# A graph network with a mixture-of-experts layer: the shared output added by accumulating scatters, and four smaller reorderings

## The chip, the core and the metric

The kernel runs on one core of one Trainium2 chip. The core has five engines, each with its own instruction stream: TensorE (PE, matrix products, with PEld for its weight loads), VectorE (DVE), ScalarE (ACT), GpSimd (POOL) and SyncE (SP). [...] SP, and here also ACT, start plain transfers by DMA; POOL starts the indirect ones (gathers and scatters by row index). All of them move data through the same 16 DMA engines.

The metric is device time in microseconds, as the median of several runs. One further execution was recorded by the hardware profiler; every duration quoted here is from that record.

## The reference

There are 625 nodes with 1024 features each and 10625 directed edges (5000 random pairs in both directions and one self-loop for each node).

```python
def sage(h, W_self, W_neigh, b):            # mean over incoming edges
    agg  = segment_sum(h[src], dst, N)
    mean = agg / max(degree, 1)[:, None]
    return h @ W_self + mean @ W_neigh + b

h = layernorm(x)
x = x + sage(relu(sage(h, *layer0)), *layer1)

f = layernorm(x)
scores = softmax(f @ gate_w.T)              # 8 experts
w = scores * (one of the two best experts)
for e in range(8):                          # 1024 -> 1408 -> 1024
    out += w[:, e] * ((silu(f @ gate_e.T) * (f @ up_e.T)) @ down_e.T)
shared = (silu(f @ sg.T) * (f @ su.T)) @ sd.T         # 1024 -> 176 -> 1024
out += sigmoid(f @ shared_gate.T) * shared
return x + out
```

All of it is in float32.

## The kernel before

The nodes are cut into five tiles of 125 rows (index `t`), the 1024 features into eight chunks of 128 (index `c`) or into two halves of 512 (`half`).

A recorder, `Rec`, takes each operation with the tiles that it reads and writes. When all are recorded it emits them in program order on each engine, and puts in front of an operation only the semaphore waits that its data need. So the order on every queue is the order of the code, SP's queue of transfers included: a transfer that waits for its buffer holds all transfers behind it on SP. The helpers `ts`, `tt`, `stt`, `copy` (VectorE, or ScalarE on request), `act` (ScalarE), `mm` and `mm_all` (TensorE), `load`, `load_rows` and `store_rows` (SP by default) record one operation each, so in the profile all VectorE `tensor_tensor` operations carry the line of `tt`, L486, and so on.

The stages, in order:

1. *Start* (L575 to L602). SP loads the edge lists, then the first tile of x, then the weights `wn0`, the other tiles, `ws0`, `wn1`. POOL makes index patterns (`iota`). VectorE turns the edge lists into float columns and normalizes the first tile (`layernorm`, whose `rsqrt` is a bit trick with three rounds of Newton's method).
2. *Counting the edges* (L606 to L769). The adjacency matrix is built by 85 products of one-hot matrices; VectorE makes each pair (`os`, `od`) in `edge_rows`, TensorE counts in `count`. A list, `plan`, mixes them by hand with the transposes of the normalized rows (`tr`) and their products with `wn0` (`rows_times`). A check value `ok_i` says whether the compact counting was exact. Each of PE, ACT and DVE reads it into a register (`read_reg`), gives its branch unit a hint of the coming switch (`hint`), and runs the switch, which holds a slow recount in one case and the normal path in the other.
3. *The two graph layers* (L783 to L827). In `sage` the second layer's result is added to x in `xr`, and the row is normalized into `xf`, which is stored to a scratch tensor `xfw` in DRAM for the experts' gathers.
4. *Shared expert and routing* (L832 to L1087). `shared_up` gives the shared expert's hidden rows and the routing logits `lg` of a tile, `shared_transpose` turns them, `shared_down` multiplies with the down weights into a PSUM bank. Its `finish` scales the bank by the sigmoid weight into one of eight half-row tiles `share` (ScalarE), adds `share` to `xr` (POOL, L863), and after the second half stores the finished rows to `out` (SP). The tiles are finished in different places of the code, three groups of them late (`early`, `later`). Between them VectorE picks the two best experts and works out each row's place in its expert's list (`dest_i`, `row_i`, `place`, `id_of`, `pr`), TensorE turns the places into row indices (`own_indices`), POOL gathers the first expert's rows from `xfw` into `rows` (zeroed before), and VectorE computes the register words (`word`) by which the engines choose among bodies for different numbers of rows.
5. *The eight experts* (L1265 to L1335). For each expert: gate and up products with `wg` (11 chunks of 1 MB), the gate, transposes, down products with `wd` (11 tiles of 512 KB), the weighting into `ys`, and an indirect scatter that adds `ys` to the rows of `out` in DRAM. SP loads the next expert's `wg` chunk by chunk as TensorE leaves the buffers, and the next expert's `wd` after the present one's down products. Each scatter waits for all scatters of the expert before; those of expert 0 wait for the stores of `out` (`out_stores`).

At the end of stage 4 each of the five engines gets a no-op that reads `cnt_i`, the largest count of an expert (L1084). It orders `cnt_i` before the register loads that stand after the experts, where an overflow path is chosen for experts with more than 512 rows.

The buffers are numbered slots of 4096 bytes in each partition. `wg` lies in slots 0 to 21, `wd` in 22 to 32. The stages before use the same slots: the shared down weights lie in 22 and 23, `share` in 24 to 27 and `pr` with its neighbours in 28 to 31, so that the first loads of expert 0's weights have to wait for the last readers of these. `ws1` was in slots 24 to 31 until the last `sage`.

Of the kernel before, what the change touches and what calls it, by code (L numbers as in the profile page):

```python
# [15 lines left out]
N = 625  # L16
# [30 lines left out]
NSLOT = 3 * FC  # L47
HEAD = 4
# [249 lines left out]
def gnn_moe(nc, x, src, dst, w_gnn0, w_gnn1, b0, b1, w_gu, w_down, ws_up, ws_down, out):  # L298
# [38 lines left out]
    nid16 = const("nid16", [TP, NT], HP)  # L337
    idx = const("idx", [128, NE, NTL], I32)
# [66 lines left out]
    p = space(slot(24), slot(28))  # L405
    share = [p(f"share{i}", [TP, BANK]) for i in range(8)]
# [12 lines left out]
    place = p("place", [TP, NT, NE])  # L419
# [120 lines left out]
    def rsqrt(lo, hi):  # L540


        h, q, r = (v[:, lo:hi] for v in (ln_h, ln_q, ln_r))
        ts(h, ln_mv[:, lo:hi, 1], EPS, 0.5, ALU.add, ALU.mult)
        ts(q.bitcast(I32), h.bitcast(I32), 1, None, ALU.logical_shift_right)
        ts(r.bitcast(I32), q.bitcast(I32), -1.0, float(0x5ef759df - 2 ** 31), ALU.mult, ALU.add)
        for _ in range(3):
            tt(q, r, h, ALU.mult)
            tt(q, q, r, ALU.mult)
            stt(r, q, -1.5, r, ALU.add, ALU.mult)  # L550
# [24 lines left out]
    load(src_i, src.rearrange("(p c) -> p c", c=EC))  # L575
    load(dst_i, dst.rearrange("(p c) -> p c", c=EC))
    load_rows(xa[:, 0, :], x[:TP, :])
    for c in range(KD):
        load(wn0[:, c, :], w_gnn0[KD + c])
# [9 lines left out]
    iota(node_f, [[TP, NT], [1, PART]], 0)  # L589
    iota(pid, [[0, 1]], 0, 1)  # L590
    iota(ident, [[1, 128]], 0)
    iota(nid, [[TP, NT]], 0, 1)
    memset(const_ones, 1.0, "POOL")
    memset(ones, 1.0, "POOL")
    copy(node16, node_f)
    copy(src_f, src_i)
    ts(dhi_i, dst_i, 830.0, None, ALU.mult)
    ts(dhi_i, dhi_i, 16, None, ALU.logical_shift_right)
    ts(dval_i, dhi_i, 3.0, 127.0, ALU.mult, ALU.add)
    ts(dval_i, dval_i, 23, None, ALU.logical_shift_left)  # L600
    copy(dst_f, dst_i)
    stt(dmod, dhi_i, -float(DIG), dst_f, ALU.mult, ALU.add)  # L602
# [34 lines left out]
    def advance(until):  # L637
        while until not in did:
            what, n = now = vector.pop(0)
            if what == "rows":  # L640
                assert n < NOH or ("count", n - NOH) in did
                edge_rows(n)
            elif what == "ln" and n == 0:
                ts(ident, ident, pid, None, ALU.is_equal)
                layernorm(hrow[0], xa[:, 0, :], 0)
                did.add(("normal", 0))
            elif what == "ln":
                for t in range(1, NT):
                    moments(xa[:, t, :], t)
                rsqrt(1, NT)  # L650
                normal(hrow[1], xa[:, 1, :], 1)
                did.add(("normal", 1))
            else:
                assert ("tr", n - 2) in did
                normal(hrow[n % 2], xa[:, n, :], n)
            did.add(now)
# [57 lines left out]
    rows_times(y0, 3, 1, h0T, wn0, "p_y")  # L714
    for eng in ("PE", "ACT", "DVE"):
        read_reg(eng, body, (eng, "count"), ok_i, 1)
    bodies = {(eng, "count"): [(1, None), (0, None)] for eng in ("PE", "ACT", "DVE")}
    hint("count", bodies, ("PE",))
    scaled(c16[:, :, :N])
    tr(NT - 1)  # L720
    rows_times(y0, NT - 1, 0, h0T, wn0, "p_y")
    hint("count", bodies, ("ACT", "DVE"))
# [54 lines left out]
    copy(nid16, nid)  # L777
    iota(power_i[:, 0, :], [[3, NE]], 127)
# [37 lines left out]
    def sage(t, half, q):  # L816
# [6 lines left out]
        if half:  # L823
            rsqrt(t, t + 1)
            for n in (0, BANK):
                normal(f[:, n:n + BANK], xr[:, t, n:n + BANK], t)
            xf_stores.append(store_rows(xfw[t * TP:(t + 1) * TP, :D], f))  # L827

# [26 lines left out]
    def shared_down(t, half, b):  # L855
        lo = half * BANK
        q, o = bank("p_downs", b)[:TP, :], xr[:, t, lo:lo + BANK]
        mm(q, [(hts[:, c, t * TP:(t + 1) * TP], wds[c][:, lo:lo + BANK]) for c in range(SC)])

        def finish():  # L860
            s = share[(2 * t + half) % len(share)]
            act(s, q, AF.Copy, scale=wt[:, t, NE:])
            k.op("POOL", lambda h: h.tensor_tensor(o, s, o, ALU.add), r=[s, o], w=[o])  # L863
            if half:
                out_stores.append(store_rows(out[t * TP:(t + 1) * TP, :], xr[:, t, :]))
        return finish
# [31 lines left out]
    early = [shared_down(0, half, half) for half in range(2)]  # L898
# [6 lines left out]
    for finish in early:  # L905
        finish()
# [55 lines left out]
    stt(place, row_i, -128.0, dest_i, ALU.mult, ALU.add)  # L962
    for j in range(NTL):
        stt(id_of[:, :, :, j], row_i, float(j), of_id, ALU.is_equal, ALU.mult)
# [84 lines left out]
    for j in range(3):  # L1049
        memset(rows[j], 0.0, "POOL")  # L1050
# [22 lines left out]
    for j in range(3, NTL):  # L1073
        memset(rows[j], 0.0, "POOL")
        gather(0, j, xf_stores)
    copy(cnt_f[:, :NE], pos[0:1, NT, :])
# [7 lines left out]
    for eng in ENGINES:  # L1084
        k.op(eng, lambda h: h.nop(), r=[cnt_i])
# [179 lines left out]
    for e in range(NE):  # L1265
# [10 lines left out]
        for s in range(SEG):  # L1276
# [25 lines left out]
            if e == s == 0:  # L1302
                for c in range(FC):
                    load(wd[c], w_down[0, c])
            if more:
                for c in range(4 * s, min(4 * s + 4, FC)):
                    load_gu(e + 1, c)
# [20 lines left out]
        if more:  # L1328
# [5 lines left out]
            for c in range(FC):  # L1334
                load(wd[c], w_down[e + 1, c])  # L1335
# [109 lines left out]
```

## Time and profile before

| | |
|---|---|
| runs | 1177.58, 1181.73, 1186.67 us (median 1181.73) |
| profiled execution: time | 1181.65 us |
| profiled execution: span of the engines' work | 1179.9 us |
| TensorE busy | 1130.6 us (96%), granted clock 0.98 in the mean |
| VectorE, ScalarE, GpSimd busy | 193.4, 99.2, 55.7 us |
| DMA | 183.82 MB, 156 GB/s in the mean |

The stages in the span: edge counting until about 110 us, the first graph layer until 219, the second until 421 (with the shared expert woven in), routing until 472, then the experts. Experts 0 to 7 begin their products at 472, 567, 608, 803, 862, 898, 1006 and 1111 us; the number of rows of an expert sets its length.

[...] A 512-column float32 product is issued each 0.43 us at the full clock and each 0.85 us at half.

In lines of a wait view, "PE p_gu L526 <- DVE dest L495: 6.7, 1, 6.7" reads: TensorE, before its products into `p_gu` at line 526, stood idle for 6.7 us in all, once, 6.7 at the longest, and what ended it last by the record was VectorE's operation at line 495 that writes `dest`. "issue" stands for idle time that nothing in the record explains. Where a line begins with two numbers, these are the start in the span and the duration, both in us.

### The profile page before, as it was taken

How to read it: one execution, taken by the hardware profiler on the slowest of the kernel's cores; microseconds unless marked ns; L12 is line 12 of the kernel's file. 1: busy time of each engine (PE TensorE's matmuls, PEld its weight loads, DVE VectorE, ACT ScalarE, POOL GpSimd, SP SyncE). 2: the span in 40 equal slices, each digit the busy share in tenths (PEclk: the TensorE clock that was granted, in tenths of full speed). 3: DMA queues.
4: the chain of work that ended last, by engine and by line, in shares of the span. 5: the costliest groups of instructions: out<-in, count | busy, mean ns of one | idle time of the engine just before them, and what ended most of it. 6: DMA issues, size and time to landing. Idle time of an engine off the chain costs nothing.

```text
span 1179.9 us, 10473 instructions
## 1 busy us (share of the span) xinstructions
PE 1130.6 (96%) x4199; PEld 637.9 (54%) x4199; DVE 193.4 (16%) x590; ACT 99.2 (8%) x199; POOL 55.7 (5%) x57
## 2 busy tenths in 40 slices
PE   6999999999999996999989999999998999999996
PEld 3555777544444542444445555444546984996452
DVE  7952000200222227001100000000010000000000
ACT  1120000000000123101010000000100000000000
POOL 0000000000000014000100000010010000000101
PEclk9999999999999986999999999999999999999998
DMA  9504000303300016873795311327879852654431
GB/s 293 226 1 147 1 1 0 105 1 106 128 17 18 18 35 214 318 320 123 270 407 230 142 74 69 117 37 271 356 272 405 355 210 60 239 219 169 107 128 24
DMA packets 38628, 183.82 MB, mean 156 GB/s; under 512 B 5449, under 2 KB 5449, under 8 KB 27066
## 3 DMA queue, kind: packets, MB, share of 16 engines
q1 hardware_dynamic: 34538, 168.27, 37.2%
q0 software_dynamic: 3920, 13.70, 4.8%
q8 instruction: 56, 0.92, 0.3%
q14 instruction: 114, 0.93, 0.2%
HBM read 170.51 MB, written 11.43 MB: 154 GB/s over the span
## 4 chain that ended last, share of the span: by engine, by line
PE 92%; DVE 3%; DMA 2%; ACT 1%; issue 1%; SPq 0%; POOL 0%; DVEq 0%; ACTq 0%; POOLq 0%
PE p_gu L526 32%; PE p_down L1230 19%; PE p_y L518 11%; PE p_sage L518 9%; PE p_h L518 9%; PE p_gu L1164 3%; PE p_gs L518 2%; DMA wd<-in_w_down_dram 2%; PE p_downs L518 2%; PE pa L623 1%; PE p_tr L569 1%; PE p_gu L569 1%; DVE ln_st L534 1%; DVE pr L482 0%; SPq L459 0%
## 5 line engine op out<-in xcount | busy, mean ns | idle before, releaser
L526 PE MATMUL p_gu<-xg,wg 128*128 128x224 f32 (+1 forms) x1056 | 263.0, 412 | 0.6 <-ACT xg L494 0.5
L526 PEld LDWEIGHTS p_gu<-xg,wg 128*128 128x128 f32 x1056 | 201.0, 191 | 61.9 <-issue 60.4
L1230 PE MATMUL p_down<-wd,ht 128*128 128x512 f32 (+1 forms) x616 | 229.8, 594 | 1.4 <-DMA wd<-in_w_down_dram 1.4
L1230 PEld LDWEIGHTS p_down<-wd,ht 128*128 128x128 f32 (+1 forms) x616 | 95.3, 175 | 126.4 <-issue 126.0
L526 PE MATMUL p_gu<-wg,xg 128*128 128x512 f32 (+1 forms) x288 | 117.5, 568 | 7.3 <-DVE dest L495 6.7
L526 PEld LDWEIGHTS p_gu<-wg,xg 128*128 128x128 f32 x288 | 55.4, 194 | 67.2 <-issue 65.2
L486 DVE TENSOR_TENSOR ht<-ht,p_gu 128x256 f32<-128x256 f32 (+3 forms) x63 | 27.4, 436 | 371.6 <-PE p_gu L526 231.9
L518 PE MATMUL p_y<-wn,h0T 128*125 128x512 f32 x160 | 72.8, 609 | 3.3 <-DVE ok L486 1.3
L518 PE MATMUL p_sage<-ws,h1T 128*125 128x512 f32 x160 | 70.3, 592 | 0.0
L518 PE MATMUL p_y<-wn,h1T 128*125 128x512 f32 x160 | 68.8, 592 | 0.0
L518 PE MATMUL p_h<-h0T,ws 128*128 128x313 f32 (+1 forms) x256 | 68.0, 425 | 0.0
L499 ACT ACTIVATE ht<-p_gu 128x256 f32<-128x256 f32 (+3 forms) x63 | 25.0, 396 | 433.4 <-PE p_gu L526 354.7
L1164 PE MATMUL p_gu<-wg,xg 128*64 128x512 f32 (+2 forms) x384 | 58.3, 461 | 0.5 <-ACT xg L494 0.5
L518 PEld LDWEIGHTS p_h<-h0T,ws 128*128 128x128 f32 x256 | 48.4, 189 | 19.3 <-issue 0.5
L518 PEld LDWEIGHTS p_y<-wn,h0T 128*125 128x125 f32 x160 | 29.8, 192 | 40.2 <-issue 34.5
L518 PEld LDWEIGHTS p_y<-wn,h1T 128*125 128x125 f32 x160 | 30.1, 188 | 38.3 <-issue 37.9
L518 PEld LDWEIGHTS p_sage<-ws,h1T 128*125 128x125 f32 x160 | 29.8, 187 | 37.5 <-issue 37.2
L1103 POOL DMA_INDIRECT out_dram<-ys,idx x13 | 20.0, 1540 | 556.3 <-DVE ys L482 278.1
L518 PE MATMUL p_sage<-y,at 125*125 125x512 f32 x100 | 44.6, 592 | 0.0
L1164 PEld LDWEIGHTS p_gu<-wg,xg 128*64 128x64 f32 x384 | 25.5, 137 | 32.2 <-issue 28.1
L518 PE MATMUL p_h<-at,y 125*128 125x313 f32 (+1 forms) x160 | 42.7, 425 | 0.0
L482 DVE TENSOR_SCALAR ys<-p_down,gw 128x512 f32<-128x512 f32 x10 | 7.5, 751 | 183.0 <-PE p_down L1230 165.4
(160 smaller groups left out, 525.6 us busy)
## 6 DMA issues: line engine op xcount, KB each, us to landing
wg<-in_w_gu_dram SPq DMA_DIRECT2D x88, 1024.0 KB, 10.7
wd<-in_w_down_dram SPq DMA_DIRECT2D x88, 512.0 KB, 14.1
wn<-in_w_gnn_dram SPq DMA_DIRECT2D x16, 512.0 KB, 14.8
ws<-in_w_gnn_dram SPq DMA_DIRECT2D x16, 512.0 KB, 19.3
xa<-in_x_dram SPq DMA_DIRECT2D x5, 448.0 KB
xr<-in_x_dram SPq DMA_DIRECT2D x5, 448.0 KB
xfw<-xf SPq DMA_DIRECT2D x5, 448.0 KB
out_dram<-xr SPq DMA_DIRECT2D x5, 448.0 KB
```

The source lines that it names most:

```text
L482: return k.op("DVE", lambda h: h.tensor_scalar(o, i, s1, None, op0=op0), r=aps, w=[o])
L486: return k.op("DVE", lambda h: h.tensor_tensor(o, a, b, op), r=[a, b], w=[o])
L499: return k.op("ACT", lambda h: h.activation(o, i, f, **kw), r=aps, w=[o])
L518: k.op("PE", lambda h, a=a, b=b, s=s, e=e: h.matmul(o, a, b, start=s, stop=e, skip_group_check=True), r=[a, b], w=[o])
L526: got = h.matmul(o if m is None else o[:, :m], a, b if m is None else b[:, :m], start=start and n == 0, stop=stop and n == len(pairs) - 1, ...
L534: k.op("DVE", lambda h, part=part, st=st: h.bn_stats(st, part), r=[part], w=[st])
L569: got = h.transpose(pt[:, c, :], i[:n, (4 * g + c) * 128:(4 * g + c + 1) * 128], ident[:n, :n])
L623: k.op("PE", lambda h, s=s: h.matmul(pa[:, s, :], o_s[:, s, :], o_d[:, :DIG], start=c == 0 and s == 0, stop=c == EC - 1 and s == NT - 1, s ...
L1103: h.indirect_dma_start(out=to, out_offset=bass.IndirectOffsetOnAxis(ap=i, axis=0), in_=y, in_offset=None, compute_op=ALU.add).then_inc(s, 16)
L1164: got = h.matmul(o, *pairs[n], start=n == 0, stop=n == len(pairs) - 1, skip_group_check=True)
L1230: got = h.matmul(o[job], *pairs[job][n], start=n == 0, stop=n == FC - 1, skip_group_check=True)
```

## The change

It has five parts.

- *The shared output.* The normalized rows' source `xr` is now stored to `out` inside `sage`, right behind the store of `xf`. `share` becomes five tiles of whole rows (slots 21 and 24 to 27), `finish` is only ScalarE's scaling, and the first tile's two halves are finished at once instead of after the last `sage`. POOL's ten additions are gone. Instead POOL issues five indirect scatters (`add_rows`) that add a `share` tile to its rows of `out`, by row numbers in `nid_i`; they wait for the stores of `out`, and the experts' scatters wait for them. They stand behind all gathers of expert 0. The zeroing of `rows` covers the last nine columns only.
- *The no-ops* that read `cnt_i` are recorded behind the last expert.
- *The start.* The first tile of x is loaded first on SP; the edge lists are loaded from ACT's queue. The preparation of the edge columns moves behind the first `layernorm` (`prepare`). POOL's large `iota` moves behind two small ones. In `rsqrt` of a single column two products become one operation. The register read of `ok_i` and its hint move behind the products of tile 4 on all three engines.
- *The down weights.* The load of the next expert's first `wg` chunk waits until the present expert's `wd` tile 7 has landed (`DOWN_FIRST`).
- *The index matrices.* `id_of` is made by two operations over 160 columns instead of four over 40, from a half-precision copy of the row numbers (`row_f`).

The order of the operations on TensorE is otherwise the same.

```diff
@@ -45,6 +45,7 @@
 NSLOT = 3 * FC
+DOWN_FIRST = 7
 HEAD = 4
@@ -335,6 +336,7 @@
     nid16 = const("nid16", [TP, NT], HP)
+    nid_i = const("nid_i", [TP, NT], I32)
     idx = const("idx", [128, NE, NTL], I32)
@@ -402,8 +404,7 @@
     hs = [p(f"hs{i}", [TP, SI]) for i in range(2)]
-    p = space(slot(24), slot(28))
-    share = [p(f"share{i}", [TP, BANK]) for i in range(8)]
+    share = [sb(f"share{i}", [TP, D], FP, slot(n)) for i, n in enumerate((21, 24, 25, 26, 27))]
     p = space(slot(22), slot(24))
@@ -416,7 +417,7 @@
     dest_i, row_i = (p(n, [TP, NT, NE], I32) for n in ("dest_i", "row_i"))
-    place = p("place", [TP, NT, NE])
+    place, row_f = p("place", [TP, NT, NE]), p("row_f", [TP, NT, NE], HP)
     m16 = p("m16", [TP, NT, NE], HP)
@@ -545,8 +546,11 @@
         for _ in range(3):
-            tt(q, r, h, ALU.mult)
-            tt(q, q, r, ALU.mult)
+            if hi - lo == 1:
+                stt(q, r, h, r, ALU.mult, ALU.mult)
+            else:
+                tt(q, r, h, ALU.mult)
+                tt(q, q, r, ALU.mult)
             stt(r, q, -1.5, r, ALU.add, ALU.mult)
@@ -572,9 +576,9 @@
-    load(src_i, src.rearrange("(p c) -> p c", c=EC))
-    load(dst_i, dst.rearrange("(p c) -> p c", c=EC))
     load_rows(xa[:, 0, :], x[:TP, :])
+    load(src_i, src.rearrange("(p c) -> p c", c=EC), "ACT")
+    load(dst_i, dst.rearrange("(p c) -> p c", c=EC), "ACT")
     for c in range(KD):
@@ -586,20 +590,22 @@
-    iota(node_f, [[TP, NT], [1, PART]], 0)
     iota(pid, [[0, 1]], 0, 1)
     iota(ident, [[1, 128]], 0)
+    iota(node_f, [[TP, NT], [1, PART]], 0)
     iota(nid, [[TP, NT]], 0, 1)
     memset(ones, 1.0, "POOL")
-    copy(node16, node_f)
-    copy(src_f, src_i)
-    ts(dhi_i, dst_i, 830.0, None, ALU.mult)
-    ts(dhi_i, dhi_i, 16, None, ALU.logical_shift_right)
-    ts(dval_i, dhi_i, 3.0, 127.0, ALU.mult, ALU.add)
-    ts(dval_i, dval_i, 23, None, ALU.logical_shift_left)
-    copy(dst_f, dst_i)
-    stt(dmod, dhi_i, -float(DIG), dst_f, ALU.mult, ALU.add)
+    def prepare():
+        copy(node16, node_f)
+        copy(src_f, src_i)
+        ts(dhi_i, dst_i, 830.0, None, ALU.mult)
+        ts(dhi_i, dhi_i, 16, None, ALU.logical_shift_right)
+        ts(dval_i, dhi_i, 3.0, 127.0, ALU.mult, ALU.add)
+        ts(dval_i, dval_i, 23, None, ALU.logical_shift_left)
+        copy(dst_f, dst_i)
+        stt(dmod, dhi_i, -float(DIG), dst_f, ALU.mult, ALU.add)
+
     ids = node16.rearrange("p t m -> p (t m)")
@@ -643,6 +649,7 @@
                 layernorm(hrow[0], xa[:, 0, :], 0)
+                prepare()
                 did.add(("normal", 0))
@@ -712,14 +719,13 @@
     rows_times(y0, 3, 1, h0T, wn0, "p_y")
+    scaled(c16[:, :, :N])
+    tr(NT - 1)
+    rows_times(y0, NT - 1, 0, h0T, wn0, "p_y")
     for eng in ("PE", "ACT", "DVE"):
     bodies = {(eng, "count"): [(1, None), (0, None)] for eng in ("PE", "ACT", "DVE")}
-    hint("count", bodies, ("PE",))
-    scaled(c16[:, :, :N])
-    tr(NT - 1)
-    rows_times(y0, NT - 1, 0, h0T, wn0, "p_y")
-    hint("count", bodies, ("ACT", "DVE"))
+    hint("count", bodies)
@@ -775,6 +781,7 @@
     copy(nid16, nid)
+    copy(nid_i, nid)
     iota(power_i[:, 0, :], [[3, NE]], 127)
@@ -825,6 +832,7 @@
             xf_stores.append(store_rows(xfw[t * TP:(t + 1) * TP, :D], f))
+            out_stores.append(store_rows(out[t * TP:(t + 1) * TP, :], xr[:, t, :]))
@@ -854,15 +862,11 @@
         lo = half * BANK
-        q, o = bank("p_downs", b)[:TP, :], xr[:, t, lo:lo + BANK]
+        q, o = bank("p_downs", b)[:TP, :], share[t][:, lo:lo + BANK]
         mm(q, [(hts[:, c, t * TP:(t + 1) * TP], wds[c][:, lo:lo + BANK]) for c in range(SC)])
         def finish():
-            s = share[(2 * t + half) % len(share)]
-            act(s, q, AF.Copy, scale=wt[:, t, NE:])
-            k.op("POOL", lambda h: h.tensor_tensor(o, s, o, ALU.add), r=[s, o], w=[o])
-            if half:
-                out_stores.append(store_rows(out[t * TP:(t + 1) * TP, :], xr[:, t, :]))
+            act(o, q, AF.Copy, scale=wt[:, t, NE:])
         return finish
@@ -895,15 +899,14 @@
     sigmoid(0, 3)
-    early = [shared_down(0, half, half) for half in range(2)]
+    for half in range(2):
+        shared_down(0, half, half)()
     sage(4, 1, bank("p_sage", 5)[:TP, :])
     last3()
-    for finish in early:
-        finish()
     shared_down(1, 0, 0)()
@@ -959,9 +962,14 @@
     ts(row_i, dest_i, 7, None, ALU.logical_shift_right)
-    stt(place, row_i, -128.0, dest_i, ALU.mult, ALU.add)
-    for j in range(NTL):
-        stt(id_of[:, :, :, j], row_i, float(j), of_id, ALU.is_equal, ALU.mult)
+    copy(row_f, row_i)
+    stt(place, row_f, -128.0, dest_i, ALU.mult, ALU.add)
+    flat = id_of.rearrange("p t e j -> p (t e) j")
+    tt(flat, row_f.rearrange("p t e -> p (t e)").unsqueeze(2).to_broadcast([TP, NT * NE, NTL]),
+       slots16[:, :NTL].unsqueeze(1).to_broadcast([TP, NT * NE, NTL]), ALU.is_equal)
+    wide = [TP, NT, NE * NTL]
+    flat = id_of.rearrange("p t e j -> p t (e j)")
+    tt(flat, flat, nid16.unsqueeze(2).to_broadcast(wide), ALU.mult)
@@ -1046,8 +1054,8 @@
-    for j in range(3):
-        memset(rows[j], 0.0, "POOL")
+    for j in range(NTL):
+        memset(rows[j][:, D:], 0.0, "POOL")
     first = gather(0, 0, xf_stores)
@@ -1071,8 +1079,14 @@
     for j in range(3, NTL):
-        memset(rows[j], 0.0, "POOL")
         gather(0, j, xf_stores)
+
+    def add_rows(t):
+        o, i = share[t], nid_i[:, t:t + 1]
+        return k.op("POOL", lambda h, s: h.indirect_dma_start(
+            out=out, out_offset=bass.IndirectOffsetOnAxis(ap=i, axis=0), in_=o, in_offset=None,
+            compute_op=ALU.add).then_inc(s, 16), r=[o, i], dma=True, after=out_stores)
+    out_stores = [add_rows(t) for t in range(NT)]
     copy(cnt_f[:, :NE], pos[0:1, NT, :])
@@ -1081,8 +1095,6 @@
         read_reg(eng, words, eng, word[0:1, 0:1], 8 ** NE - 1)
-    for eng in ENGINES:
-        k.op(eng, lambda h: h.nop(), r=[cnt_i])
     hint(0, bodies, ("ACT", "DVE"))
@@ -1300,11 +1312,10 @@
             if e == s == 0:
-                for c in range(FC):
-                    load(wd[c], w_down[0, c])
+                wd_loads = [load(wd[c], w_down[0, c]) for c in range(FC)]
             if more:
                 for c in range(4 * s, min(4 * s + 4, FC)):
-                    load_gu(e + 1, c)
+                    load_gu(e + 1, c, [wd_loads[DOWN_FIRST]] if c == 0 else ())
                 if s == 0:
@@ -1331,8 +1342,9 @@
                     ts(idx_h[:, half, :], idx[:, e + 1, :], 2.0, float(half), ALU.mult, ALU.add)
-            for c in range(FC):
-                load(wd[c], w_down[e + 1, c])
+            wd_loads = [load(wd[c], w_down[e + 1, c]) for c in range(FC)]
+    for eng in ENGINES:
+        k.op(eng, lambda h: h.nop(), r=[cnt_i])
     for i in scattered:
```

## The prediction

> **What bounds the kernel now.** I read the page first: span, engine shares, the 40 slices.
>
> ```profile
> PE   6999999999999996999989999999998999999996
> ...
> PEclk9999999999999986999999999999999999999998
> ```
>
> TensorE is busy 1130.6 of 1179.9 us, so only some 49 us of idle time and what runs at a lowered clock can be won. The slices show where: the first, slices 15 and 16 (420 to 480 us, where the granted clock dips too), one at 600 and the last. Next, whom TensorE waited for (us in total, times, longest):
>
> ```profile
> PE p_tr L569 <- DVE hrow L483: 12.0, 2, 11.8
> PE p_xg L569 <- issue: 7.3, 2, 3.7
> PE p_gu L526 <- DVE dest L495: 6.7, 1, 6.7
> PE p_downs L518 <- ACT share L499: 2.9, 1, 2.9
> PE p_idx L975 <- DVE pr L482: 2.8, 1, 2.8
> PE p_down L1230 <- DMA wd<-in_w_down_dram: 1.4, 1, 1.4
> ```
>
> The 11.8 is the start, the 6.7 the no-ops in front of expert 0 (`dest` is VectorE's last operation before they are released). Third, the chain of waits in order of time (start, us, what) between the last graph layer and expert 0:
>
> ```profile
> 428.03 1.28 ACT L499
> 429.32 0.32 ACT hs L499
> 429.64 0.59 ACT share L499
> ...
> 430.27 3.77 PE p_downs L518 x4
> 434.05 6.20 PE p_gs L518 x16
> ...
> 446.24 1.08 DVE alt L486
> ...
> 448.05 1.95 DVE row_i L482
> ...
> 452.24 3.62 PE p_downs L518 x4
> ...
> 456.03 7.18 PE p_downs L518 x8
> ```
>
> Twice the same work is slow: 16 `p_gs` take 6.20 us where others of this shape take 4.87, and 8 `p_downs` take 7.18 where the same took 3.43 at 406.87. The stretch view, cut to 1 us (TensorE busy in the second figure, the clock third from the end), says why:
>
> ```profile
> 449.00:450.00 1.00, 0.00 (x0) 0.00 (x0) 0.99 (x1) 0.00 (x0) 0.95 (x2) 1.00 0.41 21
> 450.00:451.00 1.00, 0.00 (x0) 0.00 (x0) 0.88 (x5) 0.00 (x0) 0.00 (x0) 0.62 0.01 0
> ...
> 462.00:463.00 1.00, 1.00 (x2) 0.15 (x1) 0.00 (x0) 0.00 (x0) 0.00 (x0) 0.50 0.89 328
> ```
>
> An idle gap of 2.9 us (427.4 to 430.27) halves the clock until 436.3; one of 2.8 us (448.6 to 451.4) halves it until 477.3. A gap here costs its length and several microseconds behind it.
>
> **The change part by part.** The sum is against the profiled execution: span 1179.9, time 1181.65 with what lies around it; the median shown is 1181.73, practically the same.
>
> *Start.* SP issued the two index loads (0.39 + 0.28 us and gaps) before x, so x was issued at 1.52; now at about 0.75, and the loads go to ScalarE's queue, whose first work is at 12.9. x landed 5.14 us after its issue; I keep that: 0.77 earlier. `rsqrt` on one column loses three operations, 0.19 each by their spacing: 0.58. First transpose at 10.4 instead of 11.79. The eight operations of `prepare` (2.3 us), hidden before under the wait for x, now stand behind `hrow`. They end at 12.7; seventeen pairs at 0.505 follow until 21.3, where TensorE finishes its first products at 20.9, so pairs 17 to 19 and the second layernorm (9.0 us, untouched, four columns) end at 31.8 instead of 33.0. **Gain 1.2.** SP's weight loads and the other x loads are 0.77 earlier; POOL's `ident` and `pid`, first now, are not what is late.
>
> *Register read of the count.* For VectorE and ScalarE it comes later, off the path. For TensorE the load, the hint and the switch now stand together behind the products of t = 4 (94.94 to 102.07). Before, the hint was some 8 us ahead of the switch, and the gap there (102.07 to 102.75) was ScalarE's copy. [...] `ws1` loads fill the DMA engines (share about 1.0 from 96 to 107). Nearest rows: with hint and switch together and DMA full, TensorE stood 3.69 and 3.57 us at the starts of experts 2 and 5 ("issue"), ScalarE 7.9 at expert 0; where DMA was idle, nothing showed. [...] Bounds: no loss (a small gain is excluded, the copy ends at 102.69) to 4; I take **loss 1.0**.
>
> *Shared output, first half.* `early` is finished right after the sigmoid, so ScalarE's two `share` (0.69 each) run near 409 instead of 429.5, where ScalarE idles until 426. `p_downs` (1,0) then starts at 427.42, when the transposes end, and takes 1.72; `xfT` is ready at 428.03, under it. With no gap the clock stays up: `p_gs` of t = 4 takes 4.87 and ends at 434.0, not 440.27. **Gain 6.2.**
>
> *Routing.* From there to `pr`, VectorE took 10.8 us. `wt` still waits for ScalarE's `share` at +5.1. Then POOL's additions (1.26 each) and its 128x1033 memsets (0.95 each) lay beside `wt` 0.72, `alt` 1.08, `row_i` 1.95, against 0.20 for the same 125x40 elsewhere. Additions gone and memsets cut to 9 columns, these take 0.2: 3.1 less. Four `id_of` (1.1) become `row_f` (0.2) and two of 125x160 (0.27 each, an estimate from 0.33 for 125x176): 0.35 less. First `pr` at about 441.8, `p_idx` behind TensorE's own `p_downs` at 442.2: its 2.8 us gap and clock drop disappear. `p_downs` (3,1) ends at 444.5 instead of 455.85.
>
> *Next late: the register words.* `word` came 2.9 us after the first `pr`, so at 444.7; TensorE then loads two registers. Before, word (454.0) to next matmul (456.03) was 2.0 us, hidden; now it is a gap, 444.5 to 446.6. Does the clock fall? The rows: gaps of 2.9 and 2.8 halved it, 2.5 and 2.0 us after the last matmul. [...] By the row[...] it more likely falls: 7.18, `p_idx` and `p_xg` slow as before, then the old 4.15 from `p_xg` to ScalarE's zeroed bank: 458.6, and the first expert products are slow as before. I take the row. The no-ops no longer hold TensorE; that 6.7 becomes the wait for ScalarE's shares and first zeroed bank. **From 472.1 to 458.6: 13.5, the 6.2 included.**
>
> *Scatters.* POOL issues five (1.54 each by expert scatters) behind expert 0's gathers, near 447 to 456. The gathers are ahead of them, so expand is not delayed; gather j = 3 no longer waits 11.2 us for a store. Behind them in SP's order: wg chunk 10 waits for scatter 0 (slot 21), wd 2 to 5 for the others. Landing by expert scatters: 4.4 to 11.1 us. [...] Row: all landed by 467[...]. Chunk 10 is needed about 48 us after expert 0's start (507), wd at 523. Cost 0 either way. The five pairs of `out` stores move to SP at 315 to 430, where SP waits on `xf`; the next `xfw` store is 20 us away. One cast `nid_i` (0.1) lies in idle VectorE.
>
> *Down weights first.* At expert 1, TensorE waited 1.41 for wd 10 (21.3 us after issue), mixed with expert 2's wg. Now SP holds that wg until wd 7 landed, with wd 8 to 10 already issued: 5.6 MB at about 400 GB/s, 15 us, needed after 25. **Gain 1.4.** wg of expert 2 comes some 5 us later and is used from 608 on at 11.6 us a chunk. Expert 4 to 5: wg moves from 869 to about 876, needed at 898. Expert 0: wd 7 is held by `p_idx` anyway. Other experts' wg waits longer for its buffer. The 3.7 us "issue" at expert 2 stays, DMA being still full.
>
> *No-ops at the end:* `cnt_i` is 700 us old, nothing queues behind. 0.
>
> Sum: 1.2 - 1.0 + 13.5 + 1.4 = 15.1; 1181.65 - 15.1 = 1166.5.
>
> **The rivals.**
> A, forecast, clock falls in the register gap: 1166.5. Chance 0.5.
> B, clock holds: 4.8 more, and up to 2.7 if expert 0 starts warm (its first 32 products took 16.69 against 14.0): 1159 to 1162. For it: the gap is shorter than both that lowered it[...]. Chance 0.33.
> C, TensorE meets another wait as long as the one removed: the switch into expert 0[...]. Before, this lay under the 6.7 us; ScalarE took 7.9 there. The hint has 10 us of lead, which speaks against. With up to 6.7 kept: 1173. Also here: the count switch costs its full 4. Chance 0.13.
> D, slower: the adding scatters take far longer than expert scatters, and SP, in order, stands at wg 10 and wd 2 to 5 with expert 1's wg behind. It costs from a landing after some 505; to lose the 15 us and 12 more they must last until about 530, 75 us in all. The expert scatters' 11.1 at most speaks against. About 1195. Chance 0.04.
> That the edits do nothing fails on the gap at 427 and the 6.7, both of which name the removed releaser.
>
> **How the numbers follow.** A gives 1166.5; within A the start (0.4 to 2), the switch (0 to 4) and wd (0 to 1.4) make 1163 to 1170. B reaches 1158, C 1173. The range 1158 to 1173 leaves out D, half of C and a little of B. This measurement tells about 1% (11.8 us) from no change: faster is B, A but its tail and a little of C, 0.84; within 1%, 0.12; slower 0.04.
>
> **What would show it.** TensorE's waits: `p_downs` on `share`, `p_idx` on `pr`, `p_gu` on `dest` and `p_down` on wd gone; the longest is 10.4 at `hrow`. `p_gs` of t = 4 ends 7 us earlier, at about 433; `row_i` and `alt` take 0.2; the clock is 1.0 until about 446; expert 0 starts near 457. Wrong if `p_downs` of t = 4 run at 0.43 each (B), if "issue" stands ahead of expert 0 or at 103 us (C), or if wg or wd is a releaser before expert 1 (D).

## The result and the profile after

The changed kernel takes 1172.15 us (median of 12 runs, 1168.75 to 1173.90); the kernel before, on the same chip, 1183.77 us (12 runs, 1177.58 to 1189.94). The ratio is 0.990, 95% interval 0.987 to 0.992: about 12 us, 1%. The profiled execution has a span of 1168.5 us against 1179.9, 11.4 less.

TensorE's waits in the changed kernel (us in total, times, longest):

```profile
PE p_tr L573 <- DVE hrow L484: 11.3, 2, 10.6
PE p_xg L573 <- issue: 8.3, 2, 4.5
PE p_gu L527 <- DVE gw L496: 6.7, 1, 6.7
PE p_downs L519 <- DVE pr L483: 2.0, 1, 2.0
...
PE p_down L1242 <- DMA wd<-in_w_down_dram: 1.4, 1, 1.4
```

The two waits at the shared expert (2.9 on `share`, 2.8 on `pr`) are gone, and one of 2.0 us, the register words, is new. Two that were forecast to go stand there unchanged: 6.7 us in front of expert 0 and 1.4 us for `wd`. The chain of waits (start, us, what) at the shared expert and the routing:

```profile
427.68 1.72 PE p_downs L519 x4
429.40 4.88 PE p_gs L519 x16
...
439.75 0.21 DVE alt L487
...
440.69 0.20 DVE row_i L483
...
444.59 0.16 DVE word L496
...
446.81 3.69 PE p_downs L519 x8
```

The gap at 427 is closed and the 16 `p_gs` take 4.88 us instead of 6.20. `alt` and `row_i` take 0.2 us instead of 1.08 and 1.95. After the register gap (444.80 to 446.81) the eight `p_downs` still run at full clock, 3.69 us instead of 7.18. Then the timeline before expert 0 (start, us, engine, line, operation; in brackets the idle time before it):

```profile
450.72 1.07 PE L573 MATMUL p_xg<-ident,rows 128*128 128x128 f32 x8
...
453.46 2.16 ACT L500 ACTIVATE p_gu<-ident 128x512 f32<-128x512 f32 x4
...
458.49 3.75 PE L527 MATMUL p_gu<-wg,xg 128*128 128x512 f32 x4 [6.70 <-DVE gw L496]
```

ScalarE's last zeroed bank is ready at 455.62, yet TensorE starts 2.87 us later. The gap from the last `p_xg` (451.79) is 6.70 us, as long to the digit as before (465.41 to 472.11), although the no-ops have left.

Where the 11.4 us come from, by the starts of the experts in the two chains:

| stretch | before | after | gain |
|---|---|---|---|
| up to `p_gs` of t = 3 | 421.46 | 421.74 | -0.28 |
| from there to expert 0's first product | 50.65 | 36.75 | 13.90 |
| expert 0's first product to expert 2's | 135.94 | 135.27 | 0.67 |
| expert 2's to the last down product of expert 4 | 284.98 | 284.98 | 0.00 |
| from there to expert 5's first product | 4.87 | 6.39 | -1.52 |
| expert 5's first product to expert 6's | 108.02 | 108.57 | -0.55 |
| expert 6's first product to the last scatter | 165.02 | 165.02 | 0.00 |
| last scatter to the end of the span | 8.96 | 9.78 | -0.82 |

### The profile page after: what moved, and what is told of

Its sections match the earlier page's. It is cut to its first block, busy times and chain, and to the rows that moved or that the text cites. A ratio compares the mean times of both kernels' runs of the same rounds, so it can differ in the third digit from the quotient of the medians.

```text
span 1168.5 us, 10462 instructions
## 1 busy us (share of the span) xinstructions
PE 1121.3 (96%) x4199; PEld 634.9 (54%) x4199; DVE 183.3 (16%) x572; ACT 99.3 (8%) x199; POOL 49.7 (4%) x52
## 4 chain that ended last, share of the span: by engine, by line
PE 91%; DMA 3%; DVE 2%; issue 1%; SPq 1%; ACT 1%; POOL 0%; DVEq 0%; POOLq 0%
PE p_gu L527 33%; PE p_down L1242 19%; PE p_y L519 11%; PE p_sage L519 10%; PE p_h L519 9%; PE p_gu L1176 3%; PE p_gs L519 2%; DMA wd<-in_w_down_dram 2%; DMA xa<-in_x_dram 2%; PE pa L629 1%; SPq L460 1%; PE p_downs L519 1%; DVE pr L483 1%; PE p_gu L573 1%; PE p_tr L573 1%
## 5 line engine op out<-in xcount | busy, mean ns | idle before, releaser
L519 PEld LDWEIGHTS p_h<-at,y 125*128 125x128 f32 x160 | 30.2, 189 | 11.8
```

The costliest lines, as they stand in the source:

```text
L519: k.op("PE", lambda h, a=a, b=b, s=s, e=e: h.matmul(o, a, b, start=s, stop=e, skip_group_check=True), r=[a, b], w=[o])
```

## The experiments

Twelve kernels were run. The main question was what holds TensorE for 6.7 us in both kernels: the no-ops, ScalarE's zeroed banks, or the switch into expert 0's code.

**The no-ops alone.** The kernel before, with one edit:

```diff
-    for eng in ENGINES:                       # in front of expert 0
-        k.op(eng, lambda h: h.nop(), r=[cnt_i])
...
+    for eng in ENGINES:                       # behind expert 7
+        k.op(eng, lambda h: h.nop(), r=[cnt_i])
```

> The kernel before with one edit: the five no-ops that read cnt_i stand behind the experts. Theory F (TensorE's switch into expert 0 fetches its target while the weights load, and the no-ops never were what released it): expert 0's first product still comes 6.7 us after the last p_xg transpose (end 465.4, start 472.1), the time within 0.2% of before. Rival N (the no-op behind dest held TensorE, and the changed kernel met another wait that happens to be as long): the gap shrinks to 0.6 to 4.2 us (4.2 is ScalarE's last zeroed bank at 469.2), the span is 2.5 to 6 us shorter, ratio 0.995 to 0.998.

Measured: 0.9961 (0.9942 to 0.9979) against before, span 1176.8. Of TensorE's waits in this kernel, the one in front of expert 0:

```profile
PE p_gu L526 <- ACT p_gu L499: 3.9, 1, 3.9
```

The same place in its chain (start, us, what):

```profile
466.85 2.17 ACT p_gu L499 x4
469.06 16.53 PE p_gu L526 x32
```

The gap is 3.9 us, and expert 0 starts 0.04 us behind the last of the four zeroings. Rival N is right: the no-ops did hold TensorE, for 2.8 us. So the changed kernel removed this and met something else of the same size.

**Holding the loads** (two kernels). In the first, chunks 4 to 8 of expert 0's gate and up weights wait for the last zeroed bank; in the second the five scatters of `share` do too.

```diff
-    for c in range(4, 9):
-        load_gu(0, c, [first])
     for b in (1, 2, 3, 0):
-        act(bank("p_gu", b), ...)
+        zeroed = act(bank("p_gu", b), ...)
+    for c in range(4, 9):
+        load_gu(0, c, [zeroed])
...
-            ... dma=True, after=out_stores)
+            ... dma=True, after=out_stores + [zeroed])      # second kernel only
```

> The changed kernel with the loads of expert 0's gate and up chunks 4 to 8 held until ScalarE's last zeroed bank (455.6) instead of the first gather (448.4), so that between the register words and the switch only the five scatters of share move data. Theory F (the 6.7 us before expert 0 is the switch's fetch under a full DMA): expert 0 starts at ScalarE's last zeroed bank or soon behind, 455.7 to 457 instead of 458.5, or the gap shrinks by at least 1.5 us. Rival W (TensorE waits for a semaphore of ScalarE or VectorE, which these loads do not touch): the gap stays 6.7 us, within 0.3. In both the chunks land by 475, and chunk 4 is needed at 483: no loss.

> As the one with chunks 4 to 8 held, and POOL's five scatters of share also held until ScalarE's last zeroed bank, so that the DMA is idle but for the gathers of expert 0 between 447 and 455.6. Theory F: the gap before expert 0 is the smallest of all, expert 0 starts at 455.7 to 456. Rival W: still 6.7 us. A possible cost: scatters land about 7 us later, and chunk 10 and the down weights 2 to 5 behind them on SP; these are needed only at 507 and 523: none expected.

Measured: 0.9884 (0.9843 to 0.9924) and 0.9914 (0.9889 to 0.9940), not to be told from the changed kernel. The timeline of the first:

```profile
455.75 1.95 PE L573 MATMUL p_xg<-ident,rows 128*128 128x128 f32 x8
...
459.36 2.16 ACT L500 ACTIVATE p_gu<-ident 128x512 f32<-128x512 f32 x4
...
461.58 13.75 PE L527 MATMUL p_gu<-wg,xg 128*128 128x512 f32 x26 [3.88 <-ACT p_gu L500]
```

In both kernels TensorE starts within 0.06 us of the last zeroing, gap 3.88. As theory F expects, the 2.8 us are gone. This alone does not prove F: it is one profile of each kernel, and a kernel further down (the late gathers), whose loads run, is on time as well. And the times did not fall: in both executions the clock did fall in the register gap (the eight `p_downs` took 6.75 and 7.18 us, `p_xg` 1.95), and expert 0 starts at 461.58 and 460.17.

**ScalarE's zeroings early**, alone and together with held loads and scatters:

```diff
     for finish in later:
         finish()
+    for b in range(4):
+        act(bank("p_gu", b), ...)
...
     for finish in later:
-        finish()
+        held = finish()                                   # second kernel only:
+    for c in range(4, 9):                                  # loads and scatters
+        load_gu(0, c, [held])                              # wait for held
-    for b in (1, 2, 3, 0):
-        act(bank("p_gu", b), ...)
```

> The changed kernel with ScalarE's four zeroings of TensorE's banks moved up to where ScalarE idles (about 446, behind the first three share operations), so that they no longer stand behind p_xg's copy and two share operations. Theory F (under the loading weights the switch's fetch is the later of two waits): expert 0 does not start earlier, the gap from the last p_xg transpose to the first product stays at or above 5.4 us, and the time is that of the changed kernel within 0.2%. Rival Z (the zeroed bank and what follows it on ScalarE decide): the gap shrinks to 0.7 to 1.5 us (ScalarE's copy of xg), 5 us less.

> The same early zeroing, and both expert 0's chunks 4 to 8 and the five scatters of share held until ScalarE's last share operation, some 1.9 us after its copy of xg. Theory F: with the DMA idle between the register words and the switch, and no bank to wait for, the gap in front of expert 0 shrinks to 0.7 to 2 us, expert 0 starts at 452.5 to 454 where the clock holds in the register gap (456.9 to 458 where it falls); 4 us less than the changed kernel in the profile. Rival (the switch costs its 6 us whatever the DMA does): gap 5.4 us or more.

Measured: 0.9904 (0.9865 to 0.9943) and 0.9899 (0.9836 to 0.9961), spans 1163.8 and 1159.5. The first product of expert 0 in the timeline of the kernel with early zeroing alone:

```profile
456.51 15.72 PE L527 MATMUL p_gu<-wg,xg 128*128 128x512 f32 x32 [0.68 <-ACT xg L495]
```

And in that of the kernel with held loads and scatters:

```profile
453.69 13.97 PE L527 MATMUL p_gu<-wg,xg 128*128 128x512 f32 x32 [1.37 <-DVE pr L483]
```

The second came out as F expects. Theory F missed the first: loads ran, the clock fell, and the gap was only 0.68 us. So load alone does not make the wait. One difference is the lead: with the slow `p_downs`, TensorE's hint of the switch, issued in front of them, came 9.4 us before the end of `p_xg` (446.46 to 455.83); in the changed kernel 5.0. The next experiment takes the lead away.

**The hint's lead.** The kernel with early zeroings, the hint directly in front of the switch:

```diff
-    hint(0, bodies, ("PE",))
...
-    hint(0, bodies, ("ACT", "DVE"))
+    hint(0, bodies)
```

> The kernel with the early zeroing, and TensorE's hint of the switch into expert 0 moved from in front of the eight p_downs to directly in front of the switch, as at experts 2 and 5; weights load as in the changed kernel. Theory L (the hint only helps if it has led by more than some 8.6 us under load; less lead leaves a fetch at the switch): the gap from the last p_xg transpose to the first product of expert 0 is 3.6 to 8 us, whether or not the clock falls in the register gap. Rival (the hint's lead is nothing, and the early zeroing alone shortened the gap to 0.7): the gap stays 0.7 to 1.5 us.

Measured in one execution, 1173.14 us. The timeline:

```profile
455.30 1.95 PE L573 MATMUL p_xg<-ident,rows 128*128 128x128 f32 x8
463.04 1.19 PE L527 MATMUL p_gu<-wg,xg 128*128 128x512 f32 x1 [5.80 <-DVE gw L496]
```

The gap is 5.80 us where the same program with the early hint had 0.68, the banks long zeroed and the clock low in both. That fits theory L, but does not show that lead decides: in five kernels with the early hint under load the gap is as long, 5.4 to 7.4 us. (In this execution the register gap is 1.34 us instead of 2.0, so the hint itself takes some 0.65 us there, an estimate from the two gaps.)

What differs between such executions stands in the DMA view, which lists packets of a kind `instruction` (packets, MB, share of the DMA engines' time). The changed kernel has none from 446.8, just before the `p_downs` behind the hint, to 455.5. From 455.5 to 458.5 it has one in queue `q8`:

```profile
q8 instruction: 1, 0.02, 2.0%
```

The kernel with the late gathers has the same TensorE program up to here. Its one packet from 446.9 to 455.8:

```profile
q8 instruction: 1, 0.02, 1.2%
```

The packets of `q8`, 57 of 16 KB each in the changed kernel, were taken for TensorE's by their times. Thirteen of the fourteen profiles have the hint early, and they fall into two groups. In six (early zeroing and late gathers among them) its packet comes 1.3 to 2.3 us after the first `p_downs` behind it; there TensorE starts 0.7 us at most behind the last of its other waits, as far as the traces show it. In seven (the changed kernel among them) no packet follows the hint, and one comes only at the switch. In six of these seven, expert 0 starts 2.7 to 2.9 us after that packet begins; in the seventh, with all loads held, the zeroed bank is later still.

Where loads run, the packet at the switch begins 2.7 to 4.6 us after the last `p_xg` ends; where they are held, 0.3 and 0.4 us before it. The packet takes 0.9 to 1.1 us in both cases. So under load the packet at the switch began 3 to 5 us later, in the direction that F says. Lead does not tell the two groups apart: 5.0 us was enough with the late gathers, 8.6 and 8.8 us were not with `early` finished late and without the wait on `wd`. Why a packet follows the hint in one execution and not in another is open.

**Idle DMA at the other switches.**

```diff
                 for c in range(4 * s, min(4 * s + 4, FC)):
-                    load_gu(e + 1, c, ...)
+                    if e not in (1, 4) or c < 2:
+                        load_gu(e + 1, c, ...)
...
+            if e in (1, 4):                    # behind the scatters of expert e
+                for c in range(2, FC):
+                    load_gu(e + 1, c, [now[-1]])
             wd_loads = [load(wd[c], w_down[e + 1, c]) for c in range(FC)]
```

> The changed kernel with the loads that stand around the ends of experts 1 and 4 held: the next expert's gate and up chunks 2 to 10 and its down weights are issued only after the last scatter of experts 1 and 4, so that the DMA is nearly idle when TensorE, VectorE and ScalarE switch into experts 2 and 5. Theory F: TensorE's issue time in front of p_xg of experts 2 and 5 (3.80 and 4.45 us in the changed kernel) falls below 1 us each, and the time is 5 to 8 us below the changed kernel. Rival (the 3.8 and 4.45 are not the fetch under load): they stay within 0.5 us, time unchanged; a loss if the held chunks come late, from expert 2's 617 and expert 5's 898 on.

Measured: 0.9865 (0.9833 to 0.9898), span 1161.3. The chain of the changed kernel at the starts of experts 2 and 5:

```profile
585.66 3.80 issue
...
878.74 4.45 issue
```

The same two places in the chain of this kernel:

```profile
588.20 1.11 issue
...
877.35 1.35 issue
```

Both stalls shrink by about 3 us. TensorE's instruction packets at the start of expert 2, in the changed kernel from 584.5 to 589.4 and in this one from 584.5 to 588.2:

```profile
q8 instruction: 2, 0.03, 3.9%
q8 instruction: 2, 0.03, 4.3%
```

Under load the second packet begins 0.4 us after the last product of expert 1 ends, here 2.0 us before it; from there to the first transpose it is 3.4 and 3.1 us. Nothing comes late: from expert 0's first product to expert 2's it takes 131.50 us instead of 135.27, from expert 4's last down product to expert 5's first product 2.66 instead of 6.39. The span gains 7.2 although expert 0 starts 2.4 us later in this execution. The timed runs show some 4 us, with intervals that overlap, where 5 to 8 were expected. The two profiles are the clearest evidence for F: same switches, same hints, only the load on the DMA differs. What they show is the stall and the packets' times; that the stall is a fetch is the author's reading. The last kernel below repeats it.

**`early` finished late**, as before:

```diff
-    for half in range(2):
-        shared_down(0, half, half)()
+    early = [shared_down(0, half, half) for half in range(2)]
...
     last3()
+    for finish in early:
+        finish()
```

> The changed kernel with one part undone: ScalarE's two share operations of the first half are again finished behind last3, as before. If the gap of 2.9 us in front of p_downs (1,0) with its fall of the clock was worth what the prediction says: TensorE waits for share from 427.7 to about 430.3, the clock falls to 0.5 about 2 us into the gap, the 16 p_gs of t = 4 take 6.2 instead of 4.88, and p_gs ends 6 us later, as does expert 0: span 1174 to 1175. Rival: what is late next on VectorE (wt, place, word) does not depend on p_gs and takes up half or more of it: expert 0 is less than 3 us later.

Measured: 0.9949 (0.9930 to 0.9968), about 6 us slower than the changed kernel, span 1180.4. One of its waits of TensorE:

```profile
PE p_downs L519 <- ACT share L500: 2.9, 1, 2.9
```

And the chain behind it:

```profile
433.43 3.78 PE p_downs L519 x4
437.20 6.10 PE p_gs L519 x16
```

Wait, half clock and slow `p_gs` come back as before. From the start of `p_gs` of t = 3 (424.62) to the end of those of t = 4 it takes 18.68 us instead of 12.54, and no later step takes these 6.1 us up. The profiled span is 12 us longer rather than 6, since this execution also lost 2.9 us before this stage (at the count's switch, see below) and the clock fell in the register gap.

**The down weights.** One kernel drops the wait on the eighth `wd`; another holds expert 2's gathers instead:

```diff
-                    load_gu(e + 1, c, [wd_loads[DOWN_FIRST]] if c == 0 else ())
+                    load_gu(e + 1, c)                       # first kernel
...
-                        gather(e + 1, j)
+                        gather(e + 1, j, wd_loads if e == 1 and j else ())   # second
```

> The changed kernel without the wait for the eighth down weight (DOWN_FIRST) ahead of the next expert's first gate and up chunk. Theory S (SP's one queue serves its loads in order, so what is issued behind the down weights does not delay them; the down weights of expert 1 share the DMA with expert 2's gathers and expert 0's last scatter, which the wait leaves alone): TensorE's wait for wd at expert 1 stays 1.4 us within 0.4, and the time is that of the changed kernel within 0.2%. The prediction's own step (the wait frees the down weights from the next expert's chunks): the wait for wd grows to 2.8 us or stays at 1.4 with expert 2 later, and the kernel is 1.4 us or more slower.

> The changed kernel with the gathers of expert 2's rows (all but the first 128 rows) held on POOL until expert 1's down weights have landed. Theory S (1.5 MB of gathered rows are in the way of the down weights at expert 1): the last down weight lands 2 to 4 us earlier and TensorE's wait of 1.4 us for wd goes. Rival (the down weights are slow by themselves): the wait stays within 0.4 us. In both the gathered rows are needed only at 589, about 12 us after the hold.

Measured: 0.9882 (0.9824 to 0.9940) without the wait, the same as with it (0.9873 to 0.9923); TensorE's wait for `wd` is 1.9 us, 0.1 over what theory S allowed. The second took 1170.63 us in its one execution; its chain at expert 1:

```profile
555.68 16.79 DMA wd<-in_w_down_dram
...
575.97 16.15 DMA rows<-xfw,idx
```

The last `wd` lands 22.4 us after SP began to issue them (550.02) instead of 26.3, and the wait for it is gone: the gathers were in its way. But the rows now land at 592.1, and TensorE waits 4.0 us for them instead. (The trace names `rows` for another 4.0 us in front of the first transposes; the gather that these need was not held, and the stall is about as long as the switch's own, 3.80 in the changed kernel.) The expectation that they had 12 us to spare was wrong: from then on they share the DMA with the next `wg`, issued from 568.8 on.

**The count's registers** back in front of the last tile's products:

```diff
     rows_times(y0, 3, 1, h0T, wn0, "p_y")
+    for eng in ("PE", "ACT", "DVE"):
+        read_reg(eng, body, (eng, "count"), ok_i, 1)
+    bodies = ...
+    hint("count", bodies, ("PE",))
     scaled(c16[:, :, :N])
     tr(NT - 1)
     rows_times(y0, NT - 1, 0, h0T, wn0, "p_y")
-    ...
-    hint("count", bodies)
+    hint("count", bodies, ("ACT", "DVE"))
```

> The changed kernel with the count's register reads back in front of the last tile's products and TensorE's hint some 8 us ahead of its switch, as before. If the lead hides the fetch: the issue of 1.00 us at 101.7 goes (p_y of the last rows at 101.7 to 101.9), expert 0 about 0.7 to 1 us earlier, span 1 us less, below what the timed runs can tell. Rival: p_h then waits for ScalarE's copies as before (109.88) and nothing is gained.

Measured: 0.9901 (0.9868 to 0.9933). The `issue` of 1.00 us is gone: from the second layernorm's first transpose to `p_h` it takes 76.86 us, as before the change, instead of 77.57. So the move of the register reads costs 0.7 us in the changed kernel's profile, and the timed runs cannot show that. In the other nine profiles with the reads moved, the stretch varies: in four (`early` finished late, late hint, without the wait on `wd`, chunks 4 to 8 held) it takes 80.3 to 81.7 us, 3.5 to 4.9 more than before. There TensorE stands 2.8 us at this switch, and the clock falls.

**All that won, together:** early zeroings with held loads and scatters, idle DMA at experts 2 and 5, the count's registers as before.

> The changed kernel with the three edits that won by themselves or by the trace: ScalarE's zeroings early with expert 0's chunks 4 to 8 and the scatters of share held until ScalarE's last share operation; the next expert's chunks 2 to 10 and down weights held over the switches into experts 2 and 5; the count's register reads back at their old place. Theory F (each of the three switches costs what its fetch takes under load, and the savings add): expert 0 at 453 to 457, issue in front of experts 2 and 5 at 1 to 1.5 us each, none at 103 us, span 1151 to 1156, ratio to before 0.975 to 0.981, below both kernels. Rival (the savings move a wait elsewhere: held chunks or scatters come late, or the warm start of expert 0 only brings the wait for wd forward): ratio 0.984 or more.

Measured: 1158.52 us, 0.9768 (0.9742 to 0.9793) against before, better than both kernels. The ratio is in the range expected; the span, 1158.5, is 2.5 us above it. Its chain at the starts of experts 2 and 5:

```profile
585.87 1.03 issue
...
874.93 0.93 issue
```

Two things did not fit. TensorE's wait for `wd` at expert 1 is 2.6 us instead of 1.4. And the gap in front of expert 0 is 2.41 us, with the DMA idle (share 0.06 or less from 449 to 456), the banks zeroed, and a hint 9 us ahead. ScalarE's copy of `xg` ends at 454.79; the wait list has no releaser for the other 1.8 us. The instruction packets show the same as in the changed kernel: none follows the hint, the one at the switch begins at 453.88, and expert 0 starts 2.70 us later.

## Why the prediction came out as it did

The time lay in the range and the sign was right. The reasons were right for the shared output, half right for the way to expert 0, wrong for two smaller steps. By its own signs the forecast was wrong twice: the `p_downs` of t = 4 ran at the full clock (B), and "issue" stands ahead of expert 0 and at 101.7 us (C).

*Shared output, first half* (6.2): right. The profile after and the undo both show it. `p_gs` of t = 4 ended 6.0 us earlier; the "7 us" among the signs does not agree with the forecast's own sum.

*Routing*: right. `row_i` and `alt` are at 0.2, `p_idx` came at 442.46 where 442.2 was forecast, `p_downs` (3,1) ended at 444.8 for 444.5. The register gap of 2.0 us appeared, as forecast. POOL's additions and its memsets left together; which of them slowed VectorE was not tried.

*The clock in that gap*: the choice of the row, by which a gap like the two before lowers the clock, failed in the profiled execution and held in most others. In the 12 profiles with this gap the clock fell in 8, after idle times of 1.3 to 2.0 us, and stayed up in 4. The length of the gap did not tell which: 2.01 us in the changed kernel left the clock up, 1.34 us in the kernel with the late hint was followed by half clock. (The row itself was misread a little: before, the clock fell 2.4 and 1.7 us into the two gaps, not 2.5 and 2.0.)

*To expert 0* (458.6 forecast, 458.49 measured): right by luck. The clock held, which made TensorE's wait end 4.6 us earlier than forecast, and two errors of 1.6 and 2.9 us the other way cancel it. The step that failed is "that 6.7 becomes the wait for ScalarE's shares and first zeroed bank". First, the mis-sized term: TensorE waits for the last zeroed bank, not the first, 1.6 us later. On the forecast's own path, with the fallen clock, this gives 460.2, and the kernel with all loads held started at just 460.17. Second, the switch: rival C, at a chance of 0.13, is what the profiled execution shows, 2.87 us behind the last zeroing. The argument against it, that "the hint has 10 us of lead", counted on the slow `p_downs`; with the clock up the lead is 5 us. But 8.6 and 8.8 us were too little elsewhere. What the argument missed is that the hint alone assured nothing: here no packet followed it. The packet at the switch began 3.9 us after the last `p_xg`, and expert 0 started 2.85 us behind its beginning. What fills the 1.7 to 1.9 us from the end of such a packet to the first product (1.88 here) no trace shows.

*Start* (1.2): mis-sized, 0.72. The first transpose came at 10.62 as forecast (10.4), but the second layernorm waits for the last x tile, which the chain shows:

```profile
9.37 18.06 DMA xa<-in_x_dram
27.46 1.30 DVE ln_st L535 x2
```

The forecast took it for bound by VectorE's pairs; 0.5 us was lost there. *Count* (-1.0, an estimate between its bounds): right in this profile, -0.7. But the loss was 3.5 to 4.9 us in four of the ten profiles with the reads moved, where rival C had it at "its full 4" with a small chance.

*Down weights first* (1.4): wrong. The step assumed that expert 2's chunks share the DMA with `wd`. They are issued behind it on the same queue, and taking the wait away changed nothing that the runs can tell (0.9882 against 0.9898). What was in the way is another queue's traffic, the gathers: with them held, the last `wd` landed after 22.4 us instead of 26.3. The scatter beside them was not tried. (The 400 GB/s in this step are an estimate; the fullest slices of the profile before show 405 and 407.)

*Scatters* (0): right in cost. They took 23.2 to 36.7 us from issue to landing, where the expert scatters in the row had taken 4.4 to 11.1, and landed far later than the 467 of the row: SP was held until 491.8. But nothing needed what stood behind them (us in total, times, longest):

```profile
SPq L460 <- DMA out_dram<-share,nid_i: 37.6, 4, 19.2
```

*No-ops at the end* (0): the tail is 0.82 us longer, but not by them: the kernel with the no-ops alone has the old tail, 8.92. All eleven kernels built on the changed one have 9.7 to 9.8. Which part brings it was not tried.

*What the sum lacked*: the starts of experts 2 and 5 stayed at "3.7 us, issue" in the forecast; expert 5's came 1.5 us later in this execution and its body took 0.55 more. The kernels derived from the changed one need 4.8 to 6.0 us there where nothing is held, the kernel with the no-ops alone 5.3, so it is probably more scatter than effect. Of 15.1 forecast, 11.4 were realized: +0.4 to expert 0, +0.7 in its products, -0.5 at start and count, -1.4 `wd`, -2.1 at expert 5, -0.8 in the tail.

## What to carry to other kernels

TensorE's stall at a switch between code bodies depended here on what the DMA was doing. Hold prefetches that have tens of microseconds to spare until the switch is over: at two switches the stall fell from 3.80 and 4.45 us to 1.11 and 1.35. Before explaining such a stall, look for the instruction packets in the DMA view: in the changed kernel none followed the hint, and one began 2.85 us ahead of expert 0's late start. When a wait is removed, list every other thing that the same instruction waits for, with its time, and take the last, not the first; a gap that stays equally long need not have the same cause. Before ordering transfers on one queue, ask whether the competitor is on that queue at all.

## What was not expected of the hardware

Twelve profiles have the register gap, eleven of them at 2.0 us. In four the eight `p_downs` behind it ran at full clock, 3.69 us each time. In the other eight the clock fell, in six of these only after work had resumed (by 0.3 to 1.7 us; the `p_downs` took 5.55 to 6.90 us), in two within the gap (7.18 and 7.19). In all eight the 3.41 us ahead of the fall held 1.34 to 1.99 us without a product.

That length comes from the times at which the granted clock changes. In the traces of the kernel before and of the changed kernel it is 1.00 or 0.50, and all its changes within one execution lie whole multiples of 3.41 us apart (changed kernel: 455.84, 462.66, 588.96, 592.37, 882.50, 889.33). Cut at this step, the changed kernel's register gap falls into two stretches with 0.80 and 1.21 us without a product, and the clock stayed up. In the kernel before, the two gaps put 2.36 and 1.65 us without a product into the stretches ahead of the falls at 429.76 and 450.24. The step lies differently in the two executions. A length that decides does not follow: in the changed kernel the clock stayed up behind a stretch with 1.64 us (from 100.85) and behind one with 1.90 us after the last product (from 1155.57).

Where the clock fell within the gap, ScalarE's last zeroed bank came about 4.5 us later (460.1 in the kernel with all loads held, 455.6 in the changed kernel), which may be part of why the runs of the changed kernel spread over 5 us.

The five scatters of `share` take POOL 2.0 us each to issue where those of expert rows take 1.55, and a median of 28.6 us from issue to landing against 9.1.
